# A fused normalisation, attention and FFN block: the q and k projection of batches 2 to 7 as seven block products over shared sums of xn

## The chip, the cores and the metric

The kernel runs on one core of a Trainium2 chip. All operands are float32. The metric is device time in microseconds (us); the figure for a kernel is the median of several runs. A profile is one separate execution of the same program with the hardware profiler on.

## The reference, cut to what matters

Eight batches of 1024 rows with 256 channels. Each batch is normalised, and attention and FFN both read the normalised rows `xn`; both results are added to `x`. The attention is linear: per head of 16 channels `k` and `v` are first multiplied to a 16 x 16 matrix, which `q` is then multiplied with.

```python
B, N, C, H = (8, 1024, 256, 16); D = C // H
xn  = (x - mean) / sqrt(var + eps)
qkv = (xn @ qkv_w + qkv_b)                    # 256 -> 768
q, k = l2norm(q), l2norm(k)                   # over each head's 16 channels
kv  = einsum('bhnd,bhne->bhde', k, v)
att = einsum('bhnd,bhde->bhne', q, kv) @ proj_w + proj_b
ffn = relu(xn @ W1 + b1) @ W2 + b2            # 256 -> 1024 -> 256
out = x + att + ffn
```

## The kernel before

The order of every engine's instructions is written out by hand (`tc.manual_schedule()`): each engine takes its instructions in the order in which the Python code issues them, and semaphores between engines are set from the tiles that they share. DMAs are issued on SP's queue.

`v` is never computed per row. `mix_g` multiplies `xn` with the normalised `k` into a 256 x 256 matrix, `mix_kv` multiplies that with the weights of `v` and keeps the blocks on the diagonal, `mix_m` multiplies with the projection. What is left is a 256 x 256 matrix `M` by which `q` is multiplied; the FFN's second product and that one are one accumulation (`second`).

The main loop over `b` (line 679) has three stages on TensorE:

1. `hidden(b)`: the FFN's first product. It is computed as a 2 x 2 block product with seven multiplications instead of eight (Strassen's scheme in Winograd's form): both matrices are cut in four blocks, sums of blocks are made ahead (`sums_of_a` for the left side, `sums_of_b` for the right), and seven products, called a, c, d, e by the bank that they accumulate in, are combined by adds on VectorE (DVE). It runs in 12 steps, `first(i)`, `fifth(i)`, `last(i)` for four pairs of 128 output columns; small pieces of other work are put behind numbered steps (`later_steps`). After `last(i)`, GpSimd (POOL) makes the four sums of that part of the hidden layer (lines 183 to 187), which `second` needs.
2. `project(b + 1)`: q and k of the next batch, eight tiles of 128 rows by 512 columns, two matmuls each (line 310). DVE adds the bias (314), ScalarE (ACT) squares (316), DVE reduces the squares by head (319); after four tiles `norms` makes the inverse norms of q and k (333 to 335) and POOL multiplies k with them (341).
3. `second(b)`: the FFN's second product and `q` times `M`, again seven block products a, c, d, e, then a, e, d, with five matmuls each (537). `mix_g(b + 1)` (371) stands between e and the second a. Each finished block is joined with the bias (578), transposed on DVE (569), added to `x` on POOL (574) and stored.

Between the halves of `second`, the loop issues for batch `b + 1` the four sums of xn on POOL (`sums_of_x` and `s3_of_x`, which `hidden(b + 1)` reads) and `sum_of_k`, and for batch `b + 2` the normalisation and the transposition of xn (`turn_x`, DVE and 16 DMAs). The sums of one left side are s1 = a21 + a22, s2 = s1 - a11, s4 = a12 - s2, and s3 = a11 - a21, which takes a21's place.

[...] A float32 matmul of the program is two instructions on TensorE, each with its own weight load, so the 16 matmuls of `project` are x32 in the profile.

## Time and profile before

| what | value |
|---|---|
| median of 3 runs | 637.75 us (637.39 to 639.46) |
| the profiled execution's own time | 637.43 us |
| its span, first to last instruction | 635.7 us |
| busy: PE / DVE / POOL / ACT | 626.8 / 380.3 / 368.7 / 201.0 us |
| TensorE clock granted | 0.999 |
| one round of the loop on TensorE (b = 3, 4, 5) | 76.92 us |
| of it `project` / `second` with `mix_g` / `hidden` | 13.73 / 36.95 / 26.24 us |

In the profile PE is TensorE's matmul, PEld its weight load, which overlaps PE. A row of the groups reads: line, engine, operation, output<-inputs, shapes, count | busy us, mean ns of one | idle time of the engine before them and who ended it. A row of the chain or the timeline reads: start in us, duration in us, what. Two instructions on one engine overlap in their records, so the time from one start to the next is shorter than the mean of one: 32 of the matmuls of `project` have a mean of 592 ns and take 13.73 us together.

### The profile page before, as it was taken

To read this page: it belongs to the slowest core of one execution; us is meant where nothing else is said; L and a number is where in the kernel's file an instruction comes from. 1 tells how busy PE (TensorE), PEld (TensorE's weight loads), DVE (VectorE), ACT (ScalarE), POOL (GpSimd) and SP (SyncE) were. 2 spreads that over 40 slices of the span, in tenths; PEclk is the share of its full clock that TensorE was granted. 3 is DMA by queue.
4 is the path that set the end of the run, shared out by engine and by line. 5 is a ranking of instruction groups with operands and counts; after the bars stand their busy time and mean duration, and the time that the engine had idled before them with its cause. 6 is when DMAs were issued, how large, how long until landed. Compare 5 with 4: busy or idle time off the path is not lost.

```text
span 635.7 us, 5783 instructions
## 1 busy us (share of the span) xinstructions
PE 626.8 (99%) x1729; PEld 319.6 (50%) x1729; DVE 380.3 (60%) x660; ACT 201.0 (32%) x340; POOL 368.7 (58%) x309
## 2 busy tenths in 40 slices
PE   8998999999999999999999999999999999999996
PEld 5464455544645446444464444644446544555454
DVE  6795734768447663576536863467725677217833
ACT  4354303353033521244221441315313253003500
POOL 3575947387365873558553784629827298173901
PEclk9999999999999999999999999999999999999999
DMA  7714001470026400263003720047100450004202
GB/s 250 128 44 132 2 0 37 119 164 13 0 53 153 126 1 1 67 173 93 0 0 86 190 54 1 1 125 170 37 0 18 117 130 1 0 0 101 67 0 67
DMA packets 139503, 43.26 MB, mean 68 GB/s; under 512 B 135880, under 2 KB 136272, under 8 KB 139472
## 3 DMA queue, kind: packets, MB, share of 16 engines
q1 hardware_dynamic: 137296, 42.37, 26.3%
q10 hardware_dynamic: 2176, 0.52, 0.3%
q8 instruction: 14, 0.23, 0.2%
q14 instruction: 17, 0.14, 0.1%
HBM read 19.80 MB, written 8.39 MB: 44 GB/s over the span
## 4 chain that ended last, share of the span: by engine, by line
PE 96%; DVE 2%; DMA 1%; ACT 0%; issue 0%; ACTq 0%; DVEq 0%
PE pq L310 17%; PE poe L537 11%; PE poa L537 11%; PE pod L537 10%; PE gp L371 9%; PE phe L427 8%; PE pha L427 8%; PE phd L427 8%; PE poc L537 5%; PE phc L427 4%; PE kvp L388 1%; PE mp L405 1%; PE pof L537 1%; PE kvp L384 1%; DMA x<-in_L_attn_x_dram 0%; DVE hT L439 0%
## 5 line engine op out<-in xcount | busy, mean ns | idle before, releaser
L574 POOL TENSOR_TENSOR xq<-xq,yt_o 128x512 f32<-128x512 f32 x30 | 37.9, 1263 | 143.2 <-DVE yt_o L569 143.2
L310 PE MATMUL pq<-wqkv_sb,xnT 128*128 128x512 f32 x256 | 111.9, 594 | 0.3 <-ACT xnT L266 0.3
L434 ACT ACTIVATE hT<-hT,b_sb 128x512 f32<-128x512 f32 x96 | 68.6, 721 | 60.8 <-DVE hT L439 56.1
L183 POOL TENSOR_TENSOR hS<-hT 128x512 f32<-128x512 f32 x31 | 46.4, 1498 | 60.6 <-ACT hT L434 60.6
L310 PEld LDWEIGHTS pq<-wqkv_sb,xnT 128*128 128x128 f32 x256 | 49.9, 196 | 59.2 <-issue 56.4
L427 PE MATMUL pha<-xnT,w_sb 128*128 128x512 f32 x128 | 65.4, 592 | 0.0
L316 ACT ACTIVATE sq<-qk 128x512 f32<-128x512 f32 x64 | 40.3, 630 | 72.8 <-DVE ss L319 66.8
L314 DVE TENSOR_TENSOR qk<-pq,qkvb_sb 128x512 f32<-128x512 f32 x64 | 43.7, 682 | 28.6 <-PE pq L310 28.6
L537 PE MATMUL poa<-hT,w_sb 128*128 128x512 f32 x128 | 57.5, 592 | 0.0
L371 PE MATMUL gp<-qk,xn 128*128 128x256 f32 x256 | 56.6, 379 | 0.0
L371 PEld LDWEIGHTS gp<-qk,xn 128*128 128x128 f32 x256 | 48.6, 190 | 10.0 <-issue 3.8
L319 DVE TENSOR_REDUCE ss<-sq 128x32 f32<-128x512 f32 x64 | 43.5, 679 | 8.1 <-ACT sq L316 7.3
L439 DVE TENSOR_TENSOR hT<-phe,u 128x512 f32<-128x512 f32 x64 | 43.7, 684 | 7.0 <-PE phe L427 5.3
L569 DVE STREAM_TRANSPOSE yt_o<-y_o 128x512 f32<-128x512 f32 x30 | 32.9, 1096 | 16.6 <-ACT y_o L623 14.4
L341 POOL TENSOR_TENSOR qk<-qk,ss 128x1024 f32<-128x1024 f32 x16 | 30.9, 1934 | 19.3 <-DVE ss L335 14.2
L185 POOL TENSOR_TENSOR hS<-hT,hS 128x512 f32<-128x512 f32 x31 | 40.4, 1302 | 2.4
L184 POOL TENSOR_TENSOR hS<-hS,hT 128x512 f32<-128x512 f32 x31 | 40.3, 1299 | 2.4
L453 ACT COPY u<-pha 128x512 f32<-128x512 f32 x32 | 18.4, 575 | 69.1 <-PE pha L427 66.2
L187 POOL TENSOR_TENSOR hT<-hT 128x512 f32<-128x512 f32 x31 | 39.9, 1286 | 0.0
L231 ACT ACTIVATE rstd<-mv,eps_sb 128x8 f32<-128x8 f32 (+2 forms) x12 | 3.6, 299 | 110.3 <-DVE mv L229 109.1
L537 PEld LDWEIGHTS poa<-hT,w_sb 128*128 128x128 f32 x128 | 24.3, 190 | 27.6 <-issue 26.5
L277 DVE STREAM_TRANSPOSE turn_x<-xn 128x512 f32<-128x512 f32 x28 | 17.5, 681 | 33.4 <-ACT xn L251 33.4
(128 smaller groups left out, 1029.2 us busy)
## 6 DMA issues: line engine op xcount, KB each, us to landing
xq<-in_L_attn_x_dram SPq DMA_DIRECT2D x60, 128.0 KB, 3.1
out_dram<-xq SPq DMA_DIRECT2D x60, 128.0 KB, 2.4
x<-in_L_attn_x_dram SPq DMA_DIRECT2D x14, 512.0 KB, 6.3
qT<-turn_q SPq DMA_DIRECT2D x112, 64.0 KB, 2.1
xnT<-turn_x SPq DMA_DIRECT2D x104, 64.0 KB, 2.1
x<-in_L_attn_x_dram SPq DMA_DIRECT2D x4, 256.0 KB, 4.0
w_sb<-in_L_ffn_W_dram SPq DMA_DIRECT2D x2, 512.0 KB, 7.4
w_sb<-in_L_ffn_W_dram SPq DMA_DIRECT2D x8, 128.0 KB, 3.2
```

Of the source, the lines that this page charges most:

```text
L183: eng.tensor_tensor(s1, a21, a22, ALU.add)
L184: eng.tensor_tensor(s2, s1, a11, ALU.subtract)
L185: eng.tensor_tensor(s4, a12, s2, ALU.subtract)
L310: nc.tensor.matmul(pq, xnT[:, kc, t // 2, :, t % 2], wqkv_sb[:, kc, 0 : 2 * C], start=(kc == 0), stop=(kc == KC - 1),)
L314: nc.vector.tensor_tensor(qk[:, t, :], pq, qkvb_sb[:, 0 : 2 * C], ALU.add)
L316: nc.scalar.activation(sq, qk[:, t, :], AF.Square)
L319: late.append(lambda ss=ss, sq=sq, i=i: nc.vector.tensor_reduce(ss[:, i, :], sq.rearrange("p (g d) -> p g d", d=D), AX.X, ALU.add))
L371: nc.tensor.matmul(gp[:, f, :], xn[:, t, ts(f, P)], qk[:, t, C : 2 * C], start=(t == 0), stop=(t == NT - 1),)
L427: nc.tensor.matmul(dst, lhsT, rhs, start=start, stop=stop, skip_group_check=True)
L434: nc.scalar.activation(block(i, n, m), src, AF.Relu, bias=b1_sb[:, fc : fc + 1])
L439: nc.vector.tensor_tensor(dst, p, q, ALU.add)
L537: nc.tensor.matmul(dst, l, r, start=start and n == 0, stop=stop and n == len(lhs) - 1, skip_group_check=True,)
```

## The change

For batches 2 to 7 `project` is replaced by `project_by_sums`, for b = 1 to 6 in the loop. Rows are cut in halves n, input channels in halves, and the output in q and k, so that the blocks of the right side are 128 x 256; the seven products are made in two groups g of two row tiles. They read the same sums of xn as `hidden(b + 1)` does, which are therefore made earlier: s1, s2, s3 after step 10 of `hidden(b)` and s4 after step 11. The sums of the hidden layer's parts 2 and 3 are put behind them, and `sums_of_q(b)` behind these (step 11 instead of 9). The three sums of the weights and the difference of the biases (`dbias`) are made once, in the round b = 0 (`sums_of_wqk`).

q of the lower half of the rows comes out with k's bias instead of q's, and POOL adds `dbias` to it. In `project_by_sums` only k is squared, reduced and normalised; the same for q (`norms_of_q`) is issued inside `second(b)`, behind the third of its seven products. The squares' buffer becomes `yt`, `y` has one buffer instead of two, and `xS` is three tiles instead of one.

```diff
+    def sums_of_x(b, part):
+        a11, a12, a21, a22 = halves(xnTs[b])
+        if part == 0:
...
+            nc.gpsimd.tensor_tensor(s1, a21, a22, ALU.add)
+            nc.gpsimd.tensor_tensor(s2, s1, a11, ALU.subtract)
+            if b > 0:
+                s3_of_x(b)
+        else:
+            s4 = one.tile([P, HP, P, 2], F32, tag="xS4", name=f"xS4_{b}")
+            nc.gpsimd.tensor_tensor(s4, a12, xSs[b][1], ALU.subtract)
...
+    def sums_of_wqk():
+        nc.gpsimd.tensor_tensor(dbias, qkvb_sb[:, 0:C], qkvb_sb[:, C : 2 * C], ALU.subtract)
+        sums_of_b(
+            nc.gpsimd, [wqkv_sb[:, k, ts(m, C)] for k in range(2) for m in range(2)],
+            [wt[:, i, :] for i in range(3)],
+        )
+    def part_of_qk(b, n, g, m):
+        return qks[b][:, n * HT + 2 * g : n * HT + 2 * g + 2, ts(m, C)]
+    def squares_of(b, n, g, m, ss):
+        sq = work.tile([P, 2, C], F32, tag="yt", name=f"sq_{b}_{n}_{g}_{m}")
+        nc.scalar.activation(sq, part_of_qk(b, n, g, m), AF.Square)
+        return lambda: nc.vector.tensor_reduce(
+            ss[:, n * HT + 2 * g : n * HT + 2 * g + 2, :],
+            sq.rearrange("p w (g d) -> p w g d", d=D), AX.X, ALU.add,
+        )
+    def project_by_sums(b):
...
+        def mm(dst, a, rhs, g, start, stop):
+            for w in range(2):
+                nc.tensor.matmul(
+                    dst[:, w, :], a[:, g, :, w], rhs, start=start and w == 0, stop=stop,
+                    skip_group_check=True,
+                )
...
+        for g, order in enumerate(("cade", "aedc")):
+            banks.append({s: bank([P, 2, C], f"pq{s}_{b}_{g}") for s in order})
+        for g in range(2):
+            a, c_, d, e = (banks[g][s] for s in "acde")
+            mm(a, a11, b11, g, True, False)
+            u1 = add(tmp("u1", g), a, bk)
+            mm(e, s1, t1, g, True, False)
+            mm(c_, s2, t2, g, True, True)
+            u2 = add(tmp("u2", g), c_, u1)
+            u2s.append(u2)
+            mm(d, s3, t3, g, True, False)
+            u3 = add(tmp("u3", g), d, u2)
+            add(part_of_qk(b, 1, g, 1), e, u3)
+            while late:
+                late.pop(0)()
+            late.append(squares_of(b, 1, g, 1, ss))
+        for g in range(2):
+            a, c_, d, e = (banks[g][s] for s in "acde")
+            mm(a, a12, b21, g, False, True)
+            add(part_of_qk(b, 0, g, 0), a, bq)
+            mm(d, a22, t4, g, False, True)
+            add(part_of_qk(b, 1, g, 0), d, u2s[g])
+            mm(e, s4, b22, g, False, True)
+            add(part_of_qk(b, 0, g, 1), e, u2s[g])
+            while late:
+                late.pop(0)()
+            late.append(squares_of(b, 0, g, 1, ss))
+        late.pop(0)()
+        q1 = qks[b][:, HT:NT, 0:C]
+        nc.gpsimd.tensor_tensor(
+            q1, q1, dbias.unsqueeze(1).to_broadcast([P, HT, C]), ALU.add
+        )
+        invert(ss)
+        for h in range(2):
+            norms_of[b, h, 1] = ss[:, ts(h, HT), :]
+            scale(nc.gpsimd, b, h, 1)
+    def norms_of_q(b):
+        ss = small.tile([P, NT, H], F32, tag="ssq", name=f"ssq_{b}", bufs=1)
+        late = []
+        for n in range(2):
+            for g in range(2):
+                late.append(squares_of(b, n, g, 0, ss))
+                if len(late) == 2:
+                    late.pop(0)()
+        late.pop(0)()
+        invert(ss)
...
+        by_sums = 0 < b < B - 1
...
+        of_h = {3: (0,), 6: (1,), 9: () if by_sums else (2,), 11: (2, 3) if by_sums else (3,)}
         for n, step in enumerate(steps):
             step()
+            if by_sums and n == 10:
+                sums_of_x(b + 1, 0)
+            if by_sums and n == 11:
+                sums_of_x(b + 1, 1)
+            for i in of_h.get(n, ()):
+                sums_of_h(i)
             for small in small_steps.get(n, ()):
                 small()
...
-            11 if b == B - 1 else 9: [lambda: sums_of_q(b)],
+            11: [lambda: sums_of_q(b)],
...
-            pool = work if name in ("u2", "y", "yt") else one
+            pool = work if name in ("u2", "yt") else one
...
         for du, u in zip(ds, parts):
             product(du, t3, [r[:, u] for r in s3], True, False)
             add(u3[:, u], du, u2[:, u])
+        between()
         product(e, t1, s1, True, False)
...
-        if b + 1 < B:
-            project(b + 1)
-        out_parts = second(b)
-        next(out_parts)
-        if b + 1 < B:
-            sums_of_x(b + 1)
-            s3_of_x(b + 1)
-            sum_of_k(b + 1)
+        if b + 1 == 1:
+            project(1)
+            out_parts = second(b)
+        elif b + 1 < B:
+            project_by_sums(b + 1)
+            out_parts = second(b, lambda: norms_of_q(b + 1))
+        else:
+            out_parts = second(b)
+        next(out_parts)
+        if b + 1 == 1:
+            sums_of_x(1, 0)
+            sums_of_x(1, 1)
+            sums_of_wqk()
+        if b + 1 < B:
+            sum_of_k(b + 1)
```

More of the change, by code (lines that the diff above doesn't have):

```diff
@@ L208, in halves @@
         return [tt[:, k, ts(n, HP), :, :] for n in range(2) for k in range(2)]
-    def sums_of_x(b):
-        xSs[b] = one.tile([P, 3, HP, P, 2], F32, tag="xS", name=f"xS_{b}")
-        sums_of_a(nc.gpsimd, halves(xnTs[b]), *(xSs[b][:, i] for i in range(3)), s3=False)
+    def sums_of_x(b, part):
+        a11, a12, a21, a22 = halves(xnTs[b])
+        if part == 0:
+            xSs[b] = [
+                one.tile([P, HP, P, 2], F32, tag=f"xS{i}", name=f"xS{i}_{b}") for i in (1, 2)
+            ]
+            s1, s2 = xSs[b]
+            nc.gpsimd.tensor_tensor(s1, a21, a22, ALU.add)
[5 more added lines that the diff above has]
+            nc.gpsimd.tensor_tensor(s4, a12, xSs[b][1], ALU.subtract)
+            xSs[b].append(s4)
     def s3_of_x(b):
@@ L303, in project @@
         for h in range(2):
-            ss = work.tile([P, HT, 2 * H], F32, tag="ss", name=f"ss_{b}_{h}")
-            norms_of[b, h] = ss
+            ss = small.tile([P, HT, 2 * H], F32, tag="ssk" if h else "ssq", name=f"ss_{b}_{h}", bufs=1)
+            all_ss[b, h] = ss
+            for s in range(2):
+                norms_of[b, h, s] = ss[:, :, ts(s, H)]
             for i in range(HT):
@@ L314, in project @@
                 nc.vector.tensor_tensor(qk[:, t, :], pq, qkvb_sb[:, 0 : 2 * C], ALU.add)
-                sq = one.tile([P, 2 * C], F32, tag="sq", name=f"sq_{b}_{t}")
+                sq = work.tile([P, 2 * C], F32, tag="yt", name=f"sq_{b}_{t}")
                 nc.scalar.activation(sq, qk[:, t, :], AF.Square)
@@ L322, in project @@
                 if i == HT - 1 and with_norms:
-                    late.append(lambda h=h: norms(b, h))
+                    late.append(lambda h=h, ss=ss: norms(b, h, ss))
                 between.get(t, lambda: None)()
@@ L326, in project, with invert @@
             late.pop(0)()
-    norms_of = {}
-    def norms(b, h):
-        ss = norms_of[b, h]
+    norms_of, all_ss = {}, {}
+    def invert(ss):
         nc.vector.tensor_scalar_max(ss, ss, L2_EPS * L2_EPS)
@@ L335, in norms @@
         nc.vector.reciprocal(ss, ss)
+    def norms(b, h, ss):
+        invert(ss)
         scale(nc.gpsimd, b, h, 1)
+    wt = const.tile([P, 3, C], F32, tag="wt", name="wt")
+    dbias = const.tile([P, C], F32, tag="dbias", name="dbias")
+    def sums_of_wqk():
[4 more added lines that the diff above has]
+        )
@@ new lines, in part_of_qk, with add, tmp @@
+    def part_of_qk(b, n, g, m):
[8 more added lines that the diff above has]
+    def project_by_sums(b):
+        xnT, xS = xnTs[b], xSs[b]
+        qks[b] = one.tile([P, NT, 2 * C], F32, tag="qk", name=f"qk_{b}")
+        ss = small.tile([P, NT, H], F32, tag="ssk", name=f"ssk_{b}", bufs=1)
+        a11, a12, s3, a22 = halves(xnT)
+        s1, s2, s4 = xS
+        b11, t3, b21, b22 = (wqkv_sb[:, k, ts(m, C)] for k in range(2) for m in range(2))
+        t1, t2, t4 = (wt[:, i, :] for i in range(3))
+        bq, bk = (
+            qkvb_sb[:, ts(m, C)].unsqueeze(1).to_broadcast([P, 2, C]) for m in range(2)
+        )
[5 more added lines that the diff above has]
+                )
+        def add(dst, p, q):
+            nc.vector.tensor_tensor(dst, p, q, ALU.add)
+            return dst
+        def tmp(name, g):
+            pool = work if name == "u2" else one
+            return pool.tile([P, 2, C], F32, tag=name, name=f"{name}_q_{b}_{g}")
+        banks = []
+        for g, order in enumerate(("cade", "aedc")):
+            banks.append({s: bank([P, 2, C], f"pq{s}_{b}_{g}") for s in order})
+        u2s, late = [], []
+        for g in range(2):
[27 more added lines that the diff above has]
+            q1, q1, dbias.unsqueeze(1).to_broadcast([P, HT, C]), ALU.add
+        )
+        invert(ss)
+        for h in range(2):
+            norms_of[b, h, 1] = ss[:, ts(h, HT), :]
+            scale(nc.gpsimd, b, h, 1)
@@ L338, in scale @@
+    def norms_of_q(b):
[7 more added lines that the diff above has]
+        late.pop(0)()
+        invert(ss)
+        for h in range(2):
+            norms_of[b, h, 0] = ss[:, ts(h, HT), :]
     def scale(eng, b, h, s):
@@ L342, in scale @@
             part, part,
-            norms_of[b, h][:, :, ts(s, H)].unsqueeze(3).to_broadcast([P, HT, H, D]), ALU.mult,
+            norms_of[b, h, s].unsqueeze(3).to_broadcast([P, HT, H, D]), ALU.mult,
         )
@@ L422, in hidden @@
         a11, a12, s3, a22 = halves(xnT)
-        s1, s2, s4 = (xS[:, i] for i in range(3))
+        s1, s2, s4 = xS
         hSs[b] = hS = one.tile([P, 3, FH + 1, HP, P, 2], F32, tag="hS", name=f"hS_{b}")
@@ L474, in last, with sums_of_h @@
             relu(i, 0, 1, add(block(i, 0, 1), e, u2))
+        def sums_of_h(i):
             sums_of_a(
@@ L498, in first_steps @@
         return {
-            0: [lambda: load_squares(b), lambda: norms(b, 0), lambda: norms(b, 1)],
+            0: [lambda: load_squares(b)] + [lambda h=h: norms(b, h, all_ss[b, h]) for h in range(2)],
             1: [lambda: sum_of_k(b), lambda: norm_stats(b + 1, lo)],
@@ L540, in product, with second @@
             )
-    def second(b):
+    def second(b, between=lambda: None):
         xq, hT, hS, qT, (M, Mt) = xqs[b], hTs[b], hSs[b], qTs[b], Ms[b]
@@ L617, in second @@
         else:
-            y22 = tmp("y")
+            y22 = tmp("u1")
             nc.vector.scalar_tensor_tensor(y22, e, ob[:, 2, 1:2], u3, ALU.add, ALU.add)
@@ L672, in second_half @@
         nc.vector.tensor_copy(b1_sb, b1_ps)
-        sums_of_x(0)
+        sums_of_x(0, 0)
+        sums_of_x(0, 1)
     project(0, {HT - 2: second_half}, False)
```

## The prediction

> **What bounds the kernel now.** I read the page first (busy time, clock, chain), then the chain in order of time for one round, then the groups, then POOL's timeline where the sums move.

> ```profile
> PE 626.8 (99%) x1729; PEld 319.6 (50%) x1729; DVE 380.3 (60%) x660; ACT 201.0 (32%) x340; POOL 368.7 (58%) x309
> PEclk9999999999999999999999999999999999999999
> PE 96%; DVE 2%; DMA 1%; ACT 0%; issue 0%; ACTq 0%; DVEq 0%
> ...
> L341 POOL TENSOR_TENSOR qk<-qk,ss 128x1024 f32<-128x1024 f32 x16 | 30.9, 1934 | 19.3 <-DVE ss L335 14.2
> ```

> A busy PE alone proves little, since its records overlap, but the chain that ends last is 96% PE at full clock. The chain in order of time for one round shows that this is back to back:

> ```profile
> 289.33 0.86 PE pha L427 x2
> 290.19 0.86 PE phd L427 x2
> 291.04 0.86 PE phe L427 x2
> 291.90 13.73 PE pq L310 x32
> 305.63 4.29 PE poa L537 x10
> 309.93 4.29 PE poc L537 x10
> 314.22 4.29 PE pod L537 x10
> 318.51 4.29 PE poe L537 x10
> ```

> Each piece starts where the last one ends: 32 instructions of 512 columns take 13.73 us, 0.429 each, and no piece waits. The next `project` starts at 368.82, one round of 76.92 us later. So whatever shortens PE's own work shortens the kernel, as long as nothing becomes late. The price of narrow instructions is in the same kernel, in `mix_g`; the columns are the stretch, its length, and busy time of PE, PEld, DVE, ACT, POOL:

> ```profile
> 322.80:329.71 6.91, 6.91 (x34) 6.08 (x33) 5.39 (x20) 0.30 (x1) 4.67 (x4) 1.00 0.00 0
> 291.90:305.63 13.73, 13.73 (x34) 6.27 (x33) 9.87 (x15) 4.81 (x8) 11.27 (x10) 1.00 0.13 33
> ```

> 32 instructions of 256 columns take 6.91 us, 0.2159 each: half of 0.429 to within 0.7%. What fills POOL around the start of `project`:

> ```profile
> 288.17 1.27 POOL L187 TENSOR_TENSOR hT<-hT 128x512 f32<-128x512 f32 x1
> 289.41 1.28 POOL L183 TENSOR_TENSOR hS<-hT 128x512 f32<-128x512 f32 x1
> 290.76 1.27 POOL L184 TENSOR_TENSOR hS<-hS,hT 128x512 f32<-128x512 f32 x1
> 292.11 1.27 POOL L185 TENSOR_TENSOR hS<-hT,hS 128x512 f32<-128x512 f32 x1
> 293.34 1.27 POOL L187 TENSOR_TENSOR hT<-hT 128x512 f32<-128x512 f32 x1
> ```

> The sums of hidden part 2 start at 289.41 and take 5.17 us (start to start 1.35, 1.35, 1.23, 1.24).

> **The change, part by part.** I count time from the start of `project`, 0 = 291.90; hidden's step 10 ends at -2.57, step 11 at 0.

> *TensorE.* Per batch it removes 8 x 2 matmuls of 512 columns (32 instructions, 13.73 us) and adds 7 products x 2 groups x 2 tiles of 256 columns, 28 matmuls, 56 instructions x 0.2159 = 12.09 us. Gain 1.64 us a batch, six batches: 9.8 us. Group 0 runs a at 0, e 0.86, c 1.73, d 2.59; group 1 the same from 3.46; the second loop a 6.91, d 7.77, e 8.64, a 9.50, d 10.36, e 11.23, end 12.09. Unknown is what more waits between shorter instructions cost. The event instructions that carry extra waits last 51 ns at line 371; six stand there over eight batches, and each `mix_g` still takes 6.91. From above: 51 ns bare on each of 28 matmuls is 1.43 us a batch, 8.6 us in all; from below nothing, since an extra wait cannot shorten a stream that already runs at its spacing. I take 0, nearest to the row of line 371.

> [...]

> *Sums of xn on POOL, moved before `project`.* s1 can start when step 10 has last read the old s1 (-2.57), and POOL comes free at -2.49 (289.41). With the spacings above: s1 done -1.2, s2 0.1, s3 1.5, s4 2.7. PE wants s1 at 0.86, s2 at 1.73, s3 at 2.59, s4 at 8.64: slack 2.1, 1.6, 1.1, 5.9 us, so no wait. Rounds 1 to 6 have the same POOL times relative to `project`. The transposed xn must now have landed by -2.57 instead of 0; its DMAs are issued between 335.1 and 346.0 and land within 3.8 us, 16 us ahead of the next round's 366.2.

> *Work queued behind them on POOL.* Hidden part 2 runs 2.7 to 7.9, part 3 to 13.0, q's sums to 18.2 (q's transposition had landed at 296.68, which is 4.8). `second` starts at 12.09; its c wants s2 of part 2 at 16.4, of part 3 about 19, of q at 12.09 + 4.29 + 3.43 = 19.8; q's s2 is done at 15.7: slack 4.1 us. d wants s3 of q at 24.1, done 18.2. Then POOL adds `dbias` (128x1024, not in the trace: between 1.93, the row of line 341 of that size with a broadcast, and 2.54, two of 1.27; I take 2.5, the dearer): 20.7; k's two scalings 3.9: 24.6. `mix_g` starts at 12.09 + 17.17 = 29.26: slack 4.6 us. `sum_of_k` follows and is wanted by `mix_kv` 20 us later. The 5.1 us of sums leave the middle of `second`.

> *DVE in the stage.* 8 bias adds become 14 adds of the same 128x512 from PSUM (682 ns, spacing 0.6, or 0.8 where one reads the other), 8 reductions become 4. Queued behind each wait in order: group 0's u3 ends about 4.3, group 1's k block 8.6, then a reduction and q11 9.8, q21 10.4, k12 11.1, a reduction, group 1's three by 13.6, two reductions 15.1, then the inverse norms (0.23 to 1.35 for the maximum, square root 0.3, reciprocal 0.95) by 17.6. What PE needs: u3 of group 1 (7.9) by 10.36, its k block by 11.23, q11's bank for `second`'s a by 12.09: the tightest slack is 2.3 us. k's norms at 17.6 are before POOL wants them (20.7). ACT's four squares replace eight; its u1 copy at 16.4 stands behind the square root, and u2 waits for c at 20.7 anyway.

> *q's norms inside `second`.* Four squares, four reductions and the inversion (2.5 + 1.35 + 0.75 + 0.95, at most 5.6 us) start on DVE after u3, about 25.8, and end by 31.4; the join of e, ready at 29.4, goes up to 2 us late. PE writes that bank again at 40.5, so nothing on PE waits. Behind it on DVE stands the normalisation of batch b + 2, whose result is wanted in the next round. q's norms are first read in the next `hidden`.

> *At nothing:* `y` with one buffer (DVE both transposes it and writes the next, in order; ACT's write comes 10 us later); the seven banks (c of group 1 reuses c of group 0, read by 3.4, wanted at 5.2); the weights' sums in round 0, 5 x 0.73 = 3.65 us on POOL ahead of `sum_of_k`, which ends at 105.3 and is wanted at 115. No DMA is added or passed.

> **Sum.** Against the profiled execution's own 637.43 us (span 635.7, 1.7 around it): 637.4 - 9.8 = 627.6. The median of the runs shown is 0.32 above that execution, so I predict 627.9 us.

> **The rivals.**

> 1. *Slower: POOL becomes the bound.* Fourteen POOL instructions now stand in a row before q's s2. One row shows what DVE can do to them: the first sum of each round (line 183, at 276.32) takes 2.26 us instead of 1.27, beside a DVE multiplication with both inputs in SBUF (line 341). If each of the 14 cost x more, c would wait 14x - 4.1 us a round. The gain is gone at x = 0.41, and beyond x = 0.43 (POOL at 1.7 us a piece) the kernel is slower by over 0.3%; at 2.26 it is 6 x (13.9 - 4.1 - 1.64) = 49 us slower, about 687. Against it: beside `project`'s adds (one input in PSUM) and reductions POOL keeps 1.26 to 1.28 us, and the added DVE work is of those two kinds. Chance 0.07.
> 2. *No difference: the narrow stream carries its waits bare*, 8.6 us, giving 636.5, within 0.3%. For it: nearly each pair of instructions has a wait. Against: the rows of line 371. Chance 0.03.
> 3. *Part of the gain goes to a wait at the start of the stage.* s3 has 1.1 us; a POOL queue 2 us late (a late ReLU ahead of the sums of part 1, say) would cost 0.9 us a round, 5 us, so 633. The same size if DVE is 3 us late. Chance 0.15.

> **How the numbers follow.** Forecast 0.75, with its own range 626.8 to 629.5 (0.2% of spread in the runs, a few tenths of a microsecond of waits a round). The range goes up into rival 3: 626.6 to 632.5, which leaves out about 2 in 10. Within 0.3% (about 1.9 us, what a measurement of this kernel can tell) are rival 2 and the edge of rival 1: 0.03; slower: 0.07; faster: 0.90.

> **What would show it.** Right: rounds of 75.3 us; `project_by_sums` 12.1 us for 56 instructions with no wait listed for PE at its line; PE busy about 617; DVE up by six adds a batch (6 x 6 x 0.68 = 25 us) less nothing in reductions of q, which only move. Wrong: PE waiting for POOL's xS in the first group or hS in c, POOL pieces over 1.5 us within `project`, or more than 12.5 us for the 56 instructions.

## The result and the profile after

The changed kernel takes 627.04 us (median of 4 runs, 626.93 to 627.19), the kernel before in the same comparison 638.42 us (637.39 to 639.46): a ratio of 0.9822, 95% interval 0.9803 to 0.9841. The prediction was 627.9 us. One thing about the runs is needed to read the small differences below: those of the kernel before lie in two groups, near 637.4 and near 639.0 us (12 of 29 in the upper one in the largest comparison), so its median moves between 637.4 and 638.4 us, while the changed kernel's runs stay within about 0.3 us. The profiled executions, 637.43 and 626.93 us, are both from the lower edge, and it is these that are compared here: 10.5 us, or 10.8 us between their spans (635.65 and 624.84; 0.3 us more than before lies outside the span).

The page of the kernel after, first the busy times, then the shares of the chain that ends last:

```profile
PE 616.5 (99%) x1873; PEld 348.0 (56%) x1873; DVE 399.7 (64%) x696; ACT 199.7 (32%) x340; POOL 385.4 (62%) x320
...
PEclk9999999999999999999999999999999999999999
...
PE 97%; DVE 1%; DMA 1%; ACT 0%; issue 0%; SPq 0%; ACTq 0%; DVEq 0%
```

TensorE still is the chain: 144 more instructions, 10.3 us less of busy time, full clock. The chain in order of time for the same round (start, duration, what), with the new stage where `project` was:

```profile
286.81 0.86 PE phe L548 x2
287.67 0.86 PE pqa L394 x4
288.53 0.86 PE pqe L394 x4
289.40 0.86 PE pqc L394 x4
290.26 0.86 PE pqd L394 x4
...
298.89 0.86 PE pqe L394 x4
299.76 4.29 PE poa L670 x10
...
362.94 0.86 PE pqa L394 x4
```

Each piece again starts where the last one ends. The stage runs from 287.67 to 299.76, 12.09 us for 56 instructions where 13.73 us stood, and the round from 287.67 to 362.94 is 75.27 us instead of 76.92. Six rounds give 6 x 1.65 = 9.9 us. The stretches of the new stage and of `mix_g` (columns: stretch, its length, then busy time and count of PE, PEld, DVE, ACT, POOL, then clock, DMA share, GB/s):

```profile
287.67:299.76 12.09, 12.09 (x57) 10.98 (x57) 9.86 (x16) 3.24 (x5) 11.78 (x11) 1.00 0.20 50
316.92:323.83 6.91, 6.91 (x34) 6.08 (x33) 5.88 (x21) 0.30 (x1) 4.23 (x4) 1.00 0.00 0
```

Weight loads are recorded in 91% of the stage (10.98 of 12.09 us), and the spacing is 0.2159 us as in `mix_g`, where they fill 88%. POOL is busy for 97% of the stage (11.78 us) and still not the bound. Its timeline shows how near that is:

```profile
285.19 1.27 POOL L219 TENSOR_TENSOR xS<-xnT 128x512 f32<-128x512 f32 x1
286.54 1.27 POOL L220 TENSOR_TENSOR xS<-xS,xnT 128x512 f32<-128x512 f32 x1
287.77 1.28 POOL L231 TENSOR_TENSOR xnT<-xnT 128x512 f32<-128x512 f32 x1
289.01 1.27 POOL L225 TENSOR_TENSOR xS<-xnT,xS 128x512 f32<-128x512 f32 x1
...
305.73 2.36 POOL L438 TENSOR_TENSOR qk<-qk,dbias 128x1024 f32<-128x1024 f32 x1
308.04 3.84 POOL L462 TENSOR_TENSOR qk<-qk,ssk 128x1024 f32<-128x1024 f32 x2
```

s3 (L231) ends at 289.0, 1.3 us into the stage, and d reads it at 290.26. The addition of `dbias` takes 2.36 us, and the two scalings of k end at 311.9, 5.0 us ahead of `mix_g` at 316.92.

The 9.9 us are not all of the 10.8. The rest lies ahead of the second projection, which the change leaves as it was: it starts at 60.20 instead of 61.11 us. TensorE's one long wait there stands in `hidden(0)`, for DVE (line of the wait <- who ended it: us in total, times, longest). In the kernel before:

```profile
PE phe L427 <- DVE hT L439: 2.1, 1, 2.1
```

and in the kernel after:

```profile
PE phe L548 <- DVE hT L560: 1.7, 1, 1.7
```

The wait is 0.4 us shorter. By TensorE's timeline the other 0.5 us are gained ahead of it: 0.1 us already at the first transposition of xn (5.89 instead of 6.00), 0.3 us in the first projection, whose last 20 instructions take 8.70 instead of 9.00 us, and 0.1 us in `hidden(0)`.

### The profile page after: what moved, and what is told of

Read it like the earlier page. It is cut to its first block, busy times and chain, and to the rows that moved or that the text cites. A ratio compares the mean times of both kernels' runs of the same rounds, so it can differ in the third digit from the quotient of the medians.

```text
span 624.8 us, 6180 instructions
## 1 busy us (share of the span) xinstructions
PE 616.5 (99%) x1873; PEld 348.0 (56%) x1873; DVE 399.7 (64%) x696; ACT 199.7 (32%) x340; POOL 385.4 (62%) x320
## 4 chain that ended last, share of the span: by engine, by line
PE 97%; DVE 1%; DMA 1%; ACT 0%; issue 0%; SPq 0%; ACTq 0%; DVEq 0%
PE poe L670 11%; PE poa L670 11%; PE pod L670 10%; PE gp L492 9%; PE phe L548 9%; PE pha L548 9%; PE phd L548 8%; PE poc L670 5%; PE pq L326 4%; PE phc L548 4%; PE pqa L394 3%; PE pqd L394 3%; PE pqe L394 3%; PE pqc L394 2%; PE kvp L509 1%; PE mp L526 1%
## 5 line engine op out<-in xcount | busy, mean ns | idle before, releaser
L184 POOL TENSOR_TENSOR hS<-hT 128x512 f32<-128x512 f32 x31 | 46.5, 1499 | 60.7 <-ACT hT L555 60.7
L372 ACT ACTIVATE sq<-qk 128x512 f32<-128x512 f32 x48 | 29.0, 629 | 109.1 <-DVE qk L400 59.1
L560 DVE TENSOR_TENSOR hT<-phe,u 128x512 f32<-128x512 f32 x64 | 43.7, 684 | 7.0 <-PE phe L548 5.3
L702 DVE STREAM_TRANSPOSE yt_o<-y_o 128x512 f32<-128x512 f32 x30 | 33.0, 1099 | 16.2 <-ACT y_o L757 13.9
L185 POOL TENSOR_TENSOR hS<-hS,hT 128x512 f32<-128x512 f32 x31 | 40.3, 1299 | 2.4
L574 ACT COPY u<-pha 128x512 f32<-128x512 f32 x32 | 18.4, 575 | 69.5 <-PE pha L548 66.5
L291 DVE STREAM_TRANSPOSE turn_x<-xn 128x512 f32<-128x512 f32 x28 | 17.6, 687 | 31.1 <-ACT xn L265 31.1
L548 PEld LDWEIGHTS pha<-xnT,w_sb 128*128 128x128 f32 x128 | 23.8, 190 | 23.8 <-issue 21.0
L560 DVE TENSOR_TENSOR u<-phc,u 128x512 f32<-128x512 f32 x32 | 21.8, 682 | 22.8 <-ACT u L574 15.0
L548 PE MATMUL phe<-xS,w_sb 128*128 128x512 f32 x64 | 32.8, 594 | 1.7 <-DVE hT L560 1.7
L555 ACT ACTIVATE hT<-pha,b_sb 128x512 f32<-128x512 f32 x32 | 21.8, 682 | 37.5 <-PE pha L548 32.4
L548 PE MATMUL phd<-xnT,w_sb 128*128 128x512 f32 x64 | 32.7, 592 | 0.0
L548 PE MATMUL phe<-xS,w1t 128*128 128x512 f32 x64 | 32.7, 592 | 0.0
```

What stands on the lines that cost most here:

```text
L184: eng.tensor_tensor(s1, a21, a22, ALU.add)
L185: eng.tensor_tensor(s2, s1, a11, ALU.subtract)
L548: nc.tensor.matmul(dst, lhsT, rhs, start=start, stop=stop, skip_group_check=True)
L555: nc.scalar.activation(block(i, n, m), src, AF.Relu, bias=b1_sb[:, fc : fc + 1])
L560: nc.vector.tensor_tensor(dst, p, q, ALU.add)
L702: nc.vector.transpose(yt.rearrange("p u w r c -> p u r w c"), y.rearrange("p u (s r) w -> p u r w s", r=R),)
```

## The experiments

My theory was that the time goes with TensorE's own instructions as long as POOL's new order keeps every sum ahead, and that the place of q's norms and the early sums by themselves are worth nothing. The rivals that still mattered were a price for narrow instructions with bare waits, and POOL as the near bound. The 0.9 us at the start of the kernel stood open.

### The squares' second buffer alone (on the kernel before)

```diff
-                sq = one.tile([P, 2 * C], F32, tag="sq", name=f"sq_{b}_{t}")
+                sq = work.tile([P, 2 * C], F32, tag="yt", name=f"sq_{b}_{t}")
```

> The kernel before with one edit: the squares of q and k have two buffers (the tag yt) instead of one. Theory: the changed kernel is 0.9 us earlier at the start of the second projection (60.20 us against 61.11) because in the first projection a square no longer waits for the reduction of the square before it, so that ScalarE reaches its copies of the transposed xn sooner and TensorE does not wait 0.3 us for them. Then this kernel shows the same: its second projection starts 0.4 to 0.9 us earlier than in the kernel before and the time is 0.4 to 0.9 us lower, 637.5 to 638.0 beside 638.4. Rival: the 0.9 us are chance, the first load's landing and the like; then it starts at 61.1 and the time is that of the kernel before.

Measured 636.59 us (636.4 to 638.22, 12 runs) against 637.62 us (29 runs): ratio 0.9978, 0.9969 to 0.9987. The second projection starts at 60.19 us and TensorE's wait is 1.72 us, as after the whole change. One of ScalarE's squares in the first projection, in the kernel before and then with two buffers:

```profile
15.40 0.63 ACT L316 ACTIVATE sq<-qk 128x512 f32<-128x512 f32 x1 [0.75 <-DVE ss L319]
```

```profile
14.55 0.63 ACT L316 ACTIVATE sq<-qk 128x512 f32<-128x512 f32 x1 [0.89 <-DVE qk L314]
```

The square now waits for its own input (line 314) and no longer for the reduction of the square before it (319). ScalarE's next copies of the transposed xn start at 15.09 instead of 15.94 us, and VectorE still is 0.9 us ahead at the addition that TensorE waits for (56.59 instead of 57.51). So the 0.9 us at the start belong to this edit, but for 0.1 us that stood before the first square (the first transposition starts at 5.87 instead of 6.00). The prediction had described the edit as part of the change and then left it out of the sum. With the two groups of runs in view: 11 of the 12 runs lie between 636.4 and 636.8 us and only one is higher.

### Narrow instructions alone (on the kernel before)

```diff
+                wide = 2 * C if b < 2 else C
                 for kc in range(KC):
-                    nc.tensor.matmul(
-                        pq, xnT[:, kc, t // 2, :, t % 2], wqkv_sb[:, kc, 0 : 2 * C],
...
+                    for c0 in range(0, 2 * C, wide):
+                        nc.tensor.matmul(
+                            pq[:, c0 : c0 + wide], xnT[:, kc, t // 2, :, t % 2],
+                            wqkv_sb[:, kc, c0 : c0 + wide],
...
```

> The kernel before with all eight block products, but in batches 2 to 7 each matmul of the projection of 512 columns is two of 256, so 64 instructions a batch instead of 32. Theory, narrow instructions cost half to within 0.7%: 64 x 0.2159 = 13.82 us a batch instead of 13.73, so 0.5 us more in all, 638.9 beside 638.4. Rival, the narrow form has a price of its own that the seven products hide in their gain: 51 ns bare on half of the instructions would give 1.6 us a batch and 10 us in all, 648.

Measured 638.8 us (637.83 to 639.67, 10 runs), ratio 1.0012, 1.0 to 1.0023; five runs near 637.9 and five near 639.6, the two groups again. The trace decides more sharply than the median. The chain in order of time:

```profile
138.18 13.81 PE pq L312 x64
```

64 instructions of 256 columns take 13.81 us where 32 of 512 took 13.73: 0.08 us a stage, 0.5 us in all, although twice as many instructions are issued, each with its weight load (72 loads beside 73 matmuls from 138 to 155 us). That the median is so near to the expected 638.9 us is luck: it stands between the two groups. With the 56 instructions of the new stage, which carry its own waits and keep the spacing of 0.2159 us, the rival of bare waits falls.

### The sums' place alone (on the kernel before)

```diff
-        sums_of_x(0)
+        sums_of_x(0, 0)
+        sums_of_x(0, 1)
...
+            if by_sums and n == 10:
+                sums_of_x(b + 1, 0)
+            if by_sums and n == 11:
+                sums_of_x(b + 1, 1)
...
-            sums_of_x(b + 1)
+            if b == 0:
+                sums_of_x(1, 0)
+                sums_of_x(1, 1)
             s3_of_x(b + 1)
```

> The kernel before, projection unchanged, with the sums of xn for batches 2 to 7 made at the end of the hidden stage, and the sums of the hidden layer's parts 2 and 3 and of q behind them, as in the changed kernel (the sum that takes a block's place stays where it was, since the plain projection reads that block). Theory: TensorE has no wait to lose in the kernel before and gains none, so the time is that of the kernel before, within 0.5 us: moving the sums is only what makes the seven products possible. Rival, relieving GpSimd in the middle of the second product is worth something by itself: more than 1 us faster; or the later sums of the hidden layer cost a wait: more than 1 us slower.

Measured 637.94 us (637.41 to 641.45, 10 runs), ratio 1.001, 0.9993 to 1.0027, with a span of 635.6 us in the profile. Moving POOL's work by a stage is worth nothing by itself, in either direction.

### q's norms ahead of `second` (on the kernel after)

```diff
             project_by_sums(b + 1)
-            out_parts = second(b, lambda: norms_of_q(b + 1))
+            norms_of_q(b + 1)
+            out_parts = second(b)
```

> The changed kernel, with q's squares, reductions and inverse norms issued right behind the projection, ahead of the first two adds of the second product, instead of behind its third product. Theory: these adds then wait on VectorE until GpSimd has corrected q's bias, some 25 us after the projection's start instead of 20.7, but nothing that TensorE needs comes later than it is wanted, so the time is that of the changed kernel, 627.0 within 0.3. Rival, the place of q's norms is part of what makes the change pay: TensorE waits in the second product, 1 us or more a round, 633 or more.

Measured 626.85 us (626.7 to 626.92, 5 runs), ratio 0.9827, 0.9814 to 0.984. DVE's timeline with q's norms first:

```profile
310.36 1.85 DVE L348 TENSOR_SCALAR ssq<-ssq 128x128 f32<-128x128 f32 x1
312.59 0.95 DVE L350 RECIPROCAL ssq<-ssq 128x128 f32<-128x128 f32 x1 [0.38 <-ACT ssq L349]
313.46 0.63 DVE L694 TENSOR_TENSOR u_o<-poc,u_o 128x512 f32<-128x512 f32 x1
314.19 0.69 DVE L694 TENSOR_TENSOR u_o<-pod,u_o 128x512 f32<-128x512 f32 x1
```

The join of c, which starts at 308.45 in the kernel after, starts at 313.46, 5 us late, and TensorE has no new wait. So the place of q's norms is free. That part of the change costs nothing and brings nothing.

### The sums of hidden part 2 ahead of xn's (on the kernel after)

```diff
-        of_h = {3: (0,), 6: (1,), 9: () if by_sums else (2,), 11: (2, 3) if by_sums else (3,)}
+        of_h = {3: (0,), 6: (1,), 9: (2,), 11: (3,)}
```

> The changed kernel, with the sums of the hidden layer's part 2 back at step 9, ahead of the sums of xn. Theory, GpSimd has 1.1 us to spare at the start of the projection and no more: the four sums of 5.17 us in front make s1 ready at 3.9 us after the projection's start instead of -1.2, where TensorE wants it at 0.86; s2 and s3 then come 1.35 and 1.23 apart where TensorE takes 0.86 for each product, 0.4 us more for each. Together 3.1 + 0.4 + 0.4 = 3.9 us a round, 23 us in all, about 650: slower than the kernel before. Rival, the order on GpSimd leaves slack enough: 627 to 630.

Measured 660.72 us (659.75 to 662.17, 4 runs), ratio 1.0356, 1.0332 to 1.0379: slower than the kernel before. TensorE's waits:

```profile
PE pqe L394 <- POOL xS L219: 18.7, 6, 3.1
...
PE pqc L394 <- POOL xS L220: 0.4, 2, 0.2
```

The wait is the expected one to a tenth, 3.1 us in each of six rounds. But the kernel is 33.7 us slower than after the change, not 23. TensorE's timeline and, of TensorE alone, the stretches behind one of the waits (length, busy, granted clock, DMA share, GB/s) show the rest:

```profile
303.68 2.08 PE L394 MATMUL pqe<-wt,xS 128*128 128x256 f32 x4 [3.09 <-POOL xS L219]
305.54 1.51 PE L394 MATMUL pqc<-wt,xS 128*128 128x256 f32 x4
306.89 1.03 PE L394 MATMUL pqd<-wqkv_sb,xnT 128*128 128x256 f32 x4
```

```profile
303.60:305.80 2.20, 2.12 (x5) 0.50 0.37 94
305.80:307.10 1.30, 1.30 (x5) 0.72 0.17 42
307.10:316.50 9.40, 9.40 (x45) 1.00 0.00 0
```

Behind the wait the clock is at one half, and four instructions are recorded over 2.08 us instead of 1.03. Over the 12 us around each wait the mean clock is 0.86 in four rounds and 0.72 in two; with 0.50, the lowest clock that any of these stretches shows, that is by estimate 2 x 0.14 x 12 = 3.4 us and 2 x 0.28 x 12 = 6.7 us of half clock. What it costs is read from the stages, from the first pqa to the first poa: two rounds take 16.8 us, two 17.6 and two 18.4 instead of 12.09, 33 us more in all. The listed waits are 18.7 + 0.4 = 19.1 us of that. Some 14 us remain: 1.65 us each in the two rounds with 3.4 us of half clock and one wait, 2.2 us each in the two with a second wait of 0.2 us beside it, and 3.1 us each in the two with 6.7 us of half clock. Some 0.1 us of each is for starting again, as the next experiment shows. With 0.3 us ahead of the first of these stages this is all of the 33.3 us between the spans.

### One and three more pieces ahead of s1 (on the kernel after)

One piece more, 1.23 us (with three, `range(3)`):

```diff
             s1, s2 = xSs[b]
+            if b > 1:
+                for _ in range(1):
+                    nc.gpsimd.tensor_tensor(s2, a22, a11, ALU.subtract)
             nc.gpsimd.tensor_tensor(s1, a21, a22, ALU.add)
```

> The changed kernel with one more GpSimd instruction of 128x512 in front of the sums of xn in each of the six rounds (its output is overwritten). Theory of 1.1 us to spare: s3 ready at 2.8 us after the projection's start, wanted at 2.59, so 0.2 us a round, 1.2 us in all, 628.2. Rival, the spare time is larger or GpSimd is already the bound: 627.0 or 635.

> The changed kernel with three more GpSimd instructions of 128x512 in front of the sums of xn in each of the six rounds. Theory: s1 ready at 2.75 us, wanted at 0.86 (1.9 us), then 0.45 and 0.4 us at s2 and s3: 2.7 us a round, 16.5 us in all, about 643.5, which is more than the change gains. Rival, TensorE makes the time up again elsewhere: under 635.

One piece: 629.38 us (629.3 to 629.44, 4 runs), ratio 0.9863, 0.9842 to 0.9883. TensorE's timeline of that kernel:

```profile
290.00 1.03 PE L397 MATMUL pqc<-wt,xS 128*128 128x256 f32 x4
291.10 1.14 PE L397 MATMUL pqd<-wqkv_sb,xnT 128*128 128x256 f32 x4
292.07 1.03 PE L397 MATMUL pqa<-wqkv_sb,xnT 128*128 128x256 f32 x4
```

From c to d are 1.10 us instead of 0.86, from d to the next a 0.97: a wait of 0.24 us and 0.11 us for starting again, 0.35 us a round, 2.1 of the 2.4 us measured. A piece of 1.23 us that leaves 0.24 us of wait means that s3 had 1.0 us to spare, against the predicted 1.1.

Three pieces: 647.7 us (646.1 to 648.46, 4 runs), ratio 1.0147, 1.0123 to 1.017, some 4 us more than expected. TensorE's waits, then its timeline behind the second of them, then length, busy time and clock of TensorE over 9 us around the second and the third:

```profile
PE pqe L397 <- POOL xS L222: 11.5, 6, 1.9
```

```profile
219.65 1.41 PE L397 MATMUL pqe<-wt,xS 128*128 128x256 f32 x4 [1.91 <-POOL xS L222]
220.99 2.07 PE L397 MATMUL pqc<-wt,xS 128*128 128x256 f32 x4
222.86 1.49 PE L397 MATMUL pqd<-wqkv_sb,xnT 128*128 128x256 f32 x4
```

```profile
219.00:228.00 9.00, 8.35 (x30) 0.81 0.12 31
298.00:307.00 9.00, 7.74 (x33) 1.00 0.19 48
```

Waits of 1.91 to 1.94 us are followed by half clock in three of the six rounds (a mean of 0.81 over 9 us in the first, second and fourth) and by full clock in the other three (1.00). At full clock the stage takes 15.1 us, 3.0 us more than 12.09, where the expectation had 2.7. At half clock it takes 15.98, 16.11 and 16.45 us, 0.8 to 1.3 us more again. That is less than the 1.7 us that by estimate half clock for 2 x 0.19 x 9 = 3.4 us could cost; in two of these three rounds no wait for s2 is listed, which the other four rounds have (0.2 us each). The six stages are 21.4 us longer in this profile, the slowest of the four runs, 3.2 us of it by the clock; the expectation, 16.5 us, lacked these and 0.3 us a round for starting again and the later waits.

### One buffer for the squares in the kernel after

```diff
         late = []
+        sq = work.tile([P, 2 * C], F32, tag="yt", name=f"sq_{b}")
         for h in range(2):
...
-                sq = work.tile([P, 2 * C], F32, tag="yt", name=f"sq_{b}_{t}")
                 nc.scalar.activation(sq, qk[:, t, :], AF.Square)
```

In this kernel the reduction of a tile is issued behind the next square, so with one tile it reads the next tile's squares: the norms of batches 0 and 1 are formed from shifted squares.

> The changed kernel with one buffer for the squares in the projections of batches 0 and 1, as the kernel before has it. Theory: the 0.9 us that the changed kernel gained beyond the seven products come from the second buffer in the first projection; then this kernel is 0.9 us slower than the changed kernel, 627.9, and TensorE's wait in the first round is 2.1 us again instead of 1.7. If, as supposed, the spread of the kernel before (about half of its runs near 637.4, half near 639.0) is the clock dropping to half behind that wait, its runs spread again, some at 627.9 and some near 629.5. Rival, the second buffer matters only beside the unchanged projection: 627.0.

Measured 630.0 us (628.72 to 630.46, 4 runs), ratio 0.9869, 0.9846 to 0.9892: 3 us more than the kernel after, not 0.9 or 2.5. It is no plain reversal: the changed order of square and reduction brings a second wait of 1.0 us (at 31.3 to 32.3 us, far ahead of the one at 57 us), so the size of the buffer's gain is read from the first experiment. What it does show is the wait at the start, now 2.11 us, in TensorE's timeline and stretches:

```profile
59.26 1.13 PE L548 MATMUL phe<-xS,w_sb 128*128 128x512 f32 x2 [2.11 <-DVE hT L560]
60.23 3.51 PE L279 MATMUL tpq<-ident,qk 128*128 128x128 f32 x16
```

```profile
56.92:60.33 3.41, 1.30 (x4) 1.00 0.56 143
60.33:63.74 3.41, 3.41 (x18) 0.50 0.88 288
63.74:67.16 3.42, 3.42 (x9) 1.00 0.10 35
```

Behind a wait of 2.11 us the clock falls, from 60.33 to 63.74, and 16 instructions that take 1.91 us in the kernel before and after are recorded over 3.51 us. In the profiled run of the kernel before, a wait of 2.10 us at the same place is followed by a clock of 1.00. But the runs of the kernel before lie in two groups 1.5 us apart (medians of 637.5 and 639.0 in the largest comparison). That suggested the next pair.

### The wait at the start made longer, beside the kernel after once more

```diff
+    def longer():
+        sc = small.tile([P, 2 * H], F32, tag="sc", name="sc", bufs=1)
+        for _ in range(2):
+            nc.vector.tensor_reduce(
+                sc, qkvb_sb[:, 0 : 2 * C].rearrange("p (g d) -> p g d", d=D), AX.X, ALU.add
+            )
...
-            8: [lambda: turn_x(b + 1), lambda: turn_x(b + 1)],
+            8: [lambda: turn_x(b + 1), lambda: turn_x(b + 1), longer],
```

> The changed kernel once more, on the same chip as the other three, to compare them with: 627.0, spread under 0.3.

> The changed kernel with two more VectorE reductions of 128x512 behind step 8 of the first round, whose result nobody reads. They make TensorE's wait there longer, 1.7 to about 2.9 us, so 628.2 from the wait alone. Theory, a wait of TensorE of about 2 us or more can put its granted clock to half for the next few microseconds (as it did in the two kernels with a late GpSimd, where waits of 1.9 us were followed by half clock in three of six rounds and waits of 3.1 us in six of six): then nearly all runs are 1 to 2.5 us dearer still, 629.5 to 630.7, and the profile shows a granted clock under 1.0 behind the wait. Rival, the clock there has another cause: 628.2, clock 1.0.

The kernel after: 626.96 us (626.88 to 627.05, 4 runs), ratio 0.9828, 0.9812 to 0.9845, a wait of 1.72 us, and a clock of 1.00 behind it. With the wait made 3.02 us long: 629.91 us (629.83 to 631.07, 4 runs), ratio 0.9879, 0.986 to 0.9897. A wait that is 1.3 us longer costs 2.95 us (in the profiled run, the slowest, 4.1). TensorE's stretches of that kernel:

```profile
58.00:60.00 2.00, 1.51 (x2) 0.50 0.66 135
60.00:62.00 2.00, 2.00 (x9) 0.50 1.00 381
62.00:64.00 2.00, 2.00 (x11) 0.50 0.21 86
64.00:66.00 2.00, 2.00 (x5) 0.85 0.03 8
```

So the extra wait is paid about twice, and the second half of the price is the clock: in the profiled run it stays at one half from about 57.8 us (0.94 in the stretch from 56 to 58) to 64.6 us, longer than the wait itself.

### Batch 1 by sums as well

The change leaves batch 1 with the sixteen full products. This version takes it along: its weights' sums come at the start of the kernel, the bound `by_sums` begins at batch 1, and in batch 1 both groups' a and e are issued ahead of c.

```diff
-        by_sums = 0 < b < B - 1
+        by_sums = b < B - 1
...
     s3_of_x(0)
+    sums_of_wqk()
...
-        if b + 1 == 1:
-            project(1)
-            out_parts = second(b)
-        elif b + 1 < B:
+        if b + 1 < B:
             project_by_sums(b + 1)
...
-            mm(a, a11, b11, g, True, False)
+            if b > 1 or g == 0:
+                mm(a, a11, b11, g, True, False)
             u1 = add(tmp("u1", g), a, bk)
...
+            if b == 1 and g == 0:
+                mm(banks[1]["a"], a11, b11, 1, True, False)
```

> The changed kernel with batch 1 projected by seven products too: its weight sums are made behind the first batch's, the sums of the second weights one stage earlier, the first batch's transposed q is copied by VectorE instead of ScalarE, and in batch 1 both groups' products a go first, so that s1 is wanted 0.86 us later. Theory: TensorE's work is 13.73 - 12.09 = 1.64 us shorter, and the sums are ready in time (xn of batch 1 lands about 59.6, s1 at 60.9, wanted at 61.9): 627.0 - 1.6 = 625.4. Rival, GpSimd is too late in the first round, where the transposed xn lands only just ahead: no gain or up to 2 us lost.

Measured 625.89 us (625.58 to 627.36, 4 runs), ratio 0.9813, 0.9792 to 0.9833. The stage of batch 1 takes 12.13 us (60.57 to 72.70). The wait at the start is 2.1 us again, 0.4 us of the 1.6 us given back, and one of the four runs is 1.5 us above the others, with a mean clock of 0.997 where theirs is 0.999 or 1.0. I tried to shorten that wait by spreading the transpositions of xn over steps 7 to 10, which puts the first three sums of batch 1's xn one step later as well (in the first round half of the DMAs of `turn_x` are issued on ScalarE's queue, not on SP's):

```diff
-            if by_sums and n == 10:
+            if by_sums and n == 10 and b > 0:
                 sums_of_x(b + 1, 0)
             if by_sums and n == 11:
+                if b == 0:
+                    sums_of_x(b + 1, 0)
                 sums_of_x(b + 1, 1)
...
-            7: [lambda: turn_x(b + 1), lambda: turn_x(b + 1)],
-            8: [lambda: sums_of_w2(), lambda: turn_x(b + 1), lambda: turn_x(b + 1)],
-            9: [lambda: mix_m(b)],
+            7: [lambda: turn_x(b + 1)],
+            8: [lambda: sums_of_w2(), lambda: turn_x(b + 1)],
+            9: [lambda: mix_m(b), lambda: turn_x(b + 1)],
+            10: [lambda: turn_x(b + 1)],
```

> As the kernel with batch 1 projected by seven products too, and in the first round the four transpositions of batch 1's xn stand behind steps 7, 8, 9 and 10, one each, instead of two behind step 7 and two behind step 8. Theory: the one long wait of TensorE, 1.7 to 2.1 us in the first round, comes from ScalarE's queue, which issues four of these DMAs at a time (2.9 us) while a copy out of PSUM stands behind them; with two at a time the copy is 1.5 us sooner and most of the wait goes: 625.9 - 1.5 = 624.4. Rival, the transposed xn then lands later and the first product by sums waits for it instead: 625 to 627.

Measured 626.26 us (626.07 to 626.57, 4 runs), ratio 0.9818, 0.9801 to 0.9834: no gain. TensorE's waits and the POOL row behind the new one:

```profile
PE pqa L394 <- DVE qT L280: 1.5, 1, 1.5
...
PE phe L554 <- DVE hT L566: 0.7, 1, 0.7
```

```profile
60.65 1.27 POOL L219 TENSOR_TENSOR xS<-xnT 128x512 f32<-128x512 f32 x1 [0.95 <-DMA xnT<-turn_x]
```

The wait fell to 0.7 us and a new one of 1.5 us came in front of the projection, which TensorE starts at 60.65 us, at the same time as POOL its first sum. The list puts TensorE's wait down to VectorE's copies of q, which end at 60.56; POOL's first sum waits for the DMA of the last transposition, which TensorE reads as well. Which of the two held TensorE is not shown. 2.2 us wait in place of 2.1. The version that takes batch 1 along without this has the lowest median of all, 1.1 us below the kernel after; the two ratios' intervals overlap, and three of its four runs lie below all eight of the kernel after.

## Why the prediction was right, and where it was not

- *TensorE*: right, to the term. 12.09 us for 56 instructions, rounds of 75.27 us (predicted 75.3), 6 x 1.65 = 9.9 us (9.8). The price of a wait between narrow instructions was taken as nothing, and 64 narrow instructions take 0.08 us more than 32 wide ones. Weight loads are recorded in 10.98 of the 12.09 us, where they had 6.27 of 13.73, and the spacing stayed at 0.2159 us.
- *Sums of xn on POOL*: right, and the condition for all the rest. s3 was to be done 1.5 us into the stage and was done at 1.3. The spare time was to be 1.1 us, and one piece more shows 1.0. With part 2 ahead of xn's sums the whole gain is lost and more.
- *Work queued behind them on POOL*: right, with `dbias` at 2.36 us where 2.5 was taken between 1.93 and 2.54, and the scalings done 24.2 us into the stage (24.6).
- *DVE in the stage*: right where it matters. k's reciprocal ends at 304.61, 16.9 us into the stage, against at most 17.6. The 36 more adds are there: 68.7 us of adds against 43.7 in the groups, 25.0 as predicted. DVE's busy time grew by only 19.4 us; the maxima (10.7 to 9.2), the reductions (43.5 to 42.4) and the joins of e (11.3 to 10.7) shrank beside them, and the rest I did not trace.
- *q's norms inside `second`*: right. The join of e starts at 317.50, 0.6 us behind the end of e (up to 2 predicted), and nothing waits for it. Ahead of `second` they cost as little.
- *At nothing*: here is the miss. The squares' second buffer was named as part of the change and appears nowhere in the sum. The groups of the kernel before had the cost in view, 7.3 us of DVE's idle time ended by the squares, and at the start of the kernel TensorE comes to wait behind it: 0.9 us in the profiles and 1.0 us by the single edit. The sum with it is 627.9 - 1.0 = 626.9 us, against 627.04 measured. That it comes so near is in part luck: the 0.3 us that the sum adds for the spread of the runs did not come (the changed kernel's median is 0.1 us above its profiled execution), and 0.3 us more outside the span make up for it.
- *The rivals*: POOL as the bound did not come by itself, since its pieces kept to 1.26 to 1.28 us; with part 2 or three pieces put ahead it came as a wait on xS, and dearer. The loss at the start of the stage was priced as the length of the wait alone; with waits of 3.1 us ahead of s1's product the stage became 4.7 to 6.3 us longer, with waits of 1.9 us 3.0 to 4.4 us.

## What to carry to other kernels

When TensorE is back to back, a change in its instruction count can be priced from one row of the same form (here 0.2159 us an instruction in `mix_g`, and 12.09 us predicted and measured for 56), and the work goes into finding the piece on another engine with the least spare time; here 1.0 us on POOL's third sum kept 10 us. List every line of the diff against the sum, also a buffer count: it moved the one stage that did wait. And do not price a wait of TensorE at its length alone: here a stage with a wait of 1.9 us became 3.0 us longer at full clock and 3.9 to 4.4 us with half clock behind the wait, and one with a wait of 3.1 us 4.7 to 6.3 us.

## What the runs showed of the hardware

Why some waits near 2 us are followed by it and others not is not shown. Their length does not part them: behind waits of 1.91, 1.92 and 1.94 us with three pieces the clock fell, behind that of 2.14 us with batch 1 by sums it stayed at 1.00; and at the same place in the first round it fell behind 2.11 us (one buffer for the squares) and stayed behind 2.12 us (narrow instructions alone).

Had the waits of the six rounds with part 2 first, 3.1 us each, cost their own length and nothing more, their stages would have been 19 us longer; measured were 33 us.

The spread of the kernel before fits this. Its wait of 2.10 us is one of the eleven of which four were followed by half clock, and its two groups are 1.5 us apart, within the 0.8 to 3.1 us that half clock cost in the other kernels. The mean clock of every run is on record: 0.998 or 0.999 in the 17 runs of the lower group, 0.996 or 0.997 in eleven of the 12 in the upper one, and 0.993 in the slowest of all (640.89 us). By estimate 3.4 us at one half lower the mean over 636 us by 0.0027. With the wait at 1.72 us the upper group all but goes: 12 of 29 runs, then 1 of 12 (at a clock of 0.999, so from another cause), and none of the eight of the kernel after. So the upper runs lose clock; that they lose it behind this wait is argued and not shown, since none of them was profiled. If it holds, part of what the change brings in the median, up to 1 us, comes from a wait 0.4 us shorter.
